# An RWKV block with cross attention on one Trainium2 core: the four-token sums summed over channels into one row set, and the last group's output stage written as two streams

## The chip, the core and the metric

The kernel runs on one core of one Trainium2 chip (trn2). Its engines are TensorE (PE: matmuls, with the weight load PEld as a row of its own), VectorE (DVE), ScalarE (ACT), GpSimd (POOL) and SyncE (SP), whose queue issues every DMA of this kernel. The metric is the device time of one execution in microseconds. Before the change the median of three runs is 973.72 us (974.0, 972.84, 973.72).

## The reference, cut to what matters

Sixteen sequences of 128 tokens with 512 channels go through an RWKV block, 32 heads of 16 channels each, and its output through a small attention over a context:

```python
xa = _ln(x, ln1_w, ln1_b)
sx = concat([state[:, 1:2] - xa[:, :1], xa[:, :-1] - xa[:, 1:]], axis=1)
...
def step(s, rkvw):                       # 128 steps, state s: 16x16 per head
    r_t, k_t, v_t, w_t = rkvw
    a = k_t[..., :, None] * v_t[..., None, :]
    out = jnp.einsum('bhi,bhij->bhj', r_t, u * a + s)
    s = a + w_t[..., :, None] * s
    return (s, out)
...
og = ((og - m) / jnp.sqrt(va + 1e-05)).reshape(b, l, e) * gn_w + gn_b
x1 = x + og * g @ Wo.T
xc = _ln(x1, ln2_w, ln2_b)
sx2 = concat([state[:, 0:1] - xc[:, :1], xc[:, :-1] - xc[:, 1:]], axis=1)
xk2 = xc + sx2 * ffn_maa_k
xr2 = xc + sx2 * ffn_maa_r
rr = jax.nn.sigmoid(xr2 @ Wfr.T)
kk = jnp.square(jax.nn.relu(xk2 @ Wfk.T))
x2 = x1 + rr * (kk @ Wfv.T)
# second layer, x_c = x2, x_s = the context, per sequence:
Mn = conv1x1(Wn, bn, inorm(x_c));  Mm = conv1x1(Wm, bm, inorm(x_s))
A = softmax(einsum('bct,bcs->bts', Mn, Mm))
out = conv1x1(Wo, bo, einsum('bcs,bts->bct', conv1x1(Wl, bl, x_s), A)) + x_c
```

## The kernel before

Everything is fp32; a matmul or a weight load shows as two records in the trace, a transpose on TensorE as one. The 16 sequences form 8 groups (`G`) of two batch elements (`n`), b = 0 and 1. A group passes through stages written as Python generators: `stageB` (first norm, token shift), `stageB2` (the projections k, w, v, r, g), `stageR` (the recurrence), `stageC` (output product with Wo, second norm, the products with Wfk, Wfr, Wfv) and `stageL` (the attention, two generators `stageLb`, one for each b). `stageX` loads the prepared context (MV). Lines 764 to 773 run steps 0 to 11: in a step several groups stand in different stages (`OFF`), and `interleave` (L742) draws one piece at a time from the stream with the smallest key, delay (`DLY`) plus pieces drawn over pieces counted; `NEED` holds a stream back until named stages of its group are drawn. The order drawn is a priority: a scheduler behind it puts each engine's instructions, SP's DMA issues included, in a fixed order before the run, and on the chip every engine and every queue goes through its own order. So an instruction that waits holds up what is queued behind it on its engine.

**The recurrence.** `stageR` holds the 128 tokens in four blocks of 32. For every group and b, `pairs(b)` (L393 to L415) makes the products r times k of tokens within blocks of four: six VectorE products go into `PP` [128 channels, 4, 516], where the four channel blocks cc hold 8 heads each. L405 then sums the 16 channels of each head: one matmul for each cc with the constant `emat` as weights (128 rows by 32 columns, of which 8 are heads) and 512 columns of `PP`; cc's result lies in rows 32cc to 32cc+31 of `pq`, so only 8 of each 32 rows are used. L407 copies `pq` on ScalarE (128x512), L410 transposes it in four pieces of 128x128, and L412 writes it with four masked copies (one for each cc, 128x256) into the score matrix `am`. Three levels follow (`LEV`), with matmuls `pl` at L456 (32 output rows each, in four column groups of the array) and masked copies at L460 (128x512). `spread` and the `Sx` products (L489 to L493) use the same `emat` as a mask of heads. Each b's output is `y[:, b]` (L542), its sums of squares `var[:, b]` (L545). L548 to L557 make the inverse deviations of both b together: 3 + 12 small instructions and one product over 128x1024.

**The output stage.** `stageC` (L566) works on both b at once: SP loads x and the weights (`wpair`: two halves of 512 KB for each weight, tag `wc`, two buffers, so the next weight's half can only be loaded when the matmuls that use this one are through), transposes y (L578), scales it (L580), multiplies by the gate (L582). `tokmajor` (L587) runs the products with Wo, Wfr, Wfv: four matmuls of 128x512 for each b (L592). The sums into x are at L597 and L639, the second norm in `rownorm` (L141 to L145) and L205 to L208, the shifts at L609 and L150. The product with Wfk (L619) has the weight as the stationary operand and both b's tokens, 256 columns, moving. All of it uses the PSUM tag `c` (two banks). The x tile has two buffers, so x of group 7 can be loaded when group 5 is stored (L726).

**The attention.** `stageLb` (L691) makes for each of four token blocks: scores `pS` (L704), maximum (L706), exponential (L708), reciprocal (L709), scaling (L710), four transposes into `pA` (L713), a copy into `AT` (L716, one buffer for everything, two token blocks side by side), and after every second block the product `pO` (L722, 4 matmuls of 128x256) and the sum into x (L724); at the end it stores x (L726). The last group (g = 7) has the PSUM tags `c`, `lv`, `bx`, `ls`, `la` to itself by turns: scores of b = 0 in `c` and of b = 1 in `lv`, `pO` of b = 0 in `lv`.

In step 10 `stageC` of group 7 runs beside `stageL` of group 6; in step 11 `stageL` of group 7, both b, stands alone.

Of the kernel before, what the change touches and what calls it, by code (L numbers as in the profile page):

```python
# [7 lines left out]
FP = mybir.dt.float32  # L8
FPR = mybir.dt.float32r
I32 = mybir.dt.int32  # L10
AF = mybir.ActivationFunctionType
ALU = mybir.AluOpType
AX = mybir.AxisListType

B, L, E, H, S = 16, 128, 512, 32, 16
EPS = 1e-5
(V_LN1W, V_LN1B, V_MAAX, V_TD, V_U, V_GNW, V_GNB, V_LN2W, V_LN2B, V_FMK, V_FMR) = range(11)
NV = 11
n = 2
G = B // n  # L20
# [14 lines left out]
def rwkv_xattn_kernel(ctx: ExitStack, tc: tile.TileContext, a: dict, out: bass.AP):  # L35
# [28 lines left out]
    def loadxn(g):  # L64

        t = [sb.tile([128, 512], FP, name="xn") for _ in range(n)]
        for b in range(n):
# [6 lines left out]
    st = load("st", [128, 2, 4, B])  # L74
    w1 = load("maa_w1", [128, 4, 160])

    LATE = dict(td_w1=[128, 4, 64], td_w2=[128, 512], l1b=[128, 4], emat=[128, 32],
                lvm=[128, 3, 16], dgm=[128, 32])
    late = {k: const.tile(v, I32 if k in ("lvm", "dgm") else FP, name=k) for k, v in LATE.items()}
    td1, td2, l1b, emat, lvm, dgm = late.values()  # L80
# [41 lines left out]
    D = {}  # L122
# [235 lines left out]
    def stageR(g):  # L358
# [34 lines left out]
        def pairs(b):  # L393
            tt = lambda o, x, y: nc.vector.tensor_tensor(o, x, y, ALU.mult)  # L394
            tt(dg[:, :, :, 0:128:4], four(ru, b, 0, 4), four(k, b, 0, 4))
            tt(dg[:, :, 0:3, 1:129:4], four(r, b, 1, 3), four(k, b, 0, 3))
            kw = (sb if last else sb1).tile([128, 4, 2, 32], FP, name="kw", tag="xm" if last else "sq")
            tt(kw, four(k, b, 0, 2), four(w, b, 1, 2))
            tt(dg[:, :, 0:2, 2:129:4], four(r, b, 2, 2), kw)
            tt(kw[:, :, 0], kw[:, :, 0], w[:, :, b, 2:128:4])  # L400
            tt(dg[:, :, 0, 3:129:4], r[:, :, b, 3:128:4], kw[:, :, 0])

            pq = ps.tile([128, 512], FP, name="pq", **P())
            for cc in range(4):
                nc.tensor.matmul(pq[32 * cc : 32 * cc + 32], lhsT=emat, rhs=PP[:, cc, 0:512], start=True, stop=True)  # L405
            pc = sb1.tile([128, 512], FP, name="pc4", tag="gt" if last else "kt")
            nc.scalar.copy(pc, pq)  # L407
            p4 = ps.tile([128, 4, 4, 32], FP, name="p4", **P())
            for q in range(4):
                nc.tensor.transpose(p4[:, q].rearrange("p c h -> p (c h)"), pc[:, 128 * q : 128 * q + 128], ident)  # L410
            for cc in range(4):
                nc.vector.copy_predicated(  # L412
                    am[b][:, 8 * cc : 8 * cc + 8].rearrange("p h (q s) -> p h q s", s=4),
                    dgm.rearrange("p (q s) -> p q s", s=4)[:, None].to_broadcast([128, 8, 8, 4]),
                    p4[:, :, cc, 0:8].rearrange("p s h -> p h s")[:, :, None].to_broadcast([128, 8, 8, 4]))  # L415

        def expand(li):

# [52 lines left out]
        for b in range(n):  # L471
# [14 lines left out]
            def spread(c, src):  # L486

                o = Sx[:, c].rearrange("p m (a q) j -> p m a q j", a=2)
                own = emat[:, 0:8].rearrange("p (a q) -> p a q", a=2)[:, None, :, :, None].to_broadcast([128, 4, 2, 4, 16])  # L489
                nc.vector.tensor_tensor(o, src, own, ALU.mult)  # L490

            nc.vector.tensor_tensor(Sx[:, 0], s0[:, b, :, None, :].to_broadcast([128, 4, 8, 16]),
                                    emat[:, None, 0:8, None].to_broadcast([128, 4, 8, 16]), ALU.mult)  # L493
            vb = vt[:, b].rearrange("p (q x j) -> p x q j", q=4, x=8)
            yield

# [48 lines left out]
            nc.vector.tensor_reduce(var[:, b], sq.rearrange("p (h j) -> p h j", j=16), AX.X, ALU.add)  # L545
            yield

        v, t, rs = (small.tile([128, n, 32], FP, name=q, bufs=1) for q in ("gv", "gt", "gr"))  # L548
        nc.vector.tensor_scalar(v, var, 1.0 / S, EPS, ALU.mult, ALU.add)
        nc.vector.tensor_scalar(t.bitcast(I32), v.bitcast(I32), 1, None, ALU.logical_shift_right)  # L550
        nc.vector.tensor_scalar(rs.bitcast(I32), t.bitcast(I32), -1, 0x5F3759DF, ALU.mult, ALU.add)
        for _ in range(4):
            nc.vector.tensor_tensor(t, rs, rs, ALU.mult)
            nc.vector.scalar_tensor_tensor(t, t, -0.5, v, ALU.mult, ALU.mult)
            nc.vector.scalar_tensor_tensor(rs, t, 1.5, rs, ALU.add, ALU.mult)
        y4 = y.rearrange("p b (h j) -> p (b h) j", j=16)
        nc.vector.tensor_tensor(y4, y4, rs.rearrange("p b h -> p (b h)")[:, :, None].to_broadcast([128, n * 32, 16]), ALU.mult)  # L557
        d["y"] = y
        yield

# [5 lines left out]
    def stageC(g):  # L566
# [73 lines left out]
            d["ssum"][b] = su  # L640

        tokmajor("Wfv", kk, use_f)
        yield


# [107 lines left out]
                done.add(s[4])  # L753

    ST = [(stageB, 3), (stageB2, 5), (stageR, 30), (stageC, 5), (stageL, 6), (stageX, 2)]
    NEED = [(), (0,), (1,), (2,), (3, 5), (), ()]
    done = set()

    def step_of(k, g):
        if k == 5 and g == G - 1:  # L760
            return g + LASTX
        return g + OFF[k]

    for step in range(G + max(OFF)):
        streams = []
        for k in ORDER:
            for g in range(G):
                if step_of(k, g) == step:
                    streams.append((ST[k][0](g), ST[k][1], DLY[k], (k, g)))
        if step in EARLY:  # L770
            gs = EARLY[step]
            streams.append((stageE(gs), 2 * len(gs), 1, (6, step)))
        interleave(streams)


def _prep(np, inp):
# [36 lines left out]
    r["l1b"] = np.stack([L1("bn"), L1("bm"), L1("bl"), L1("bo")], axis=1)  # L813
    r["ident"] = np.eye(128, dtype=np.float32)
    p = np.arange(128)
    r["emat"] = (p[:, None] // 16 == np.arange(32)).astype(np.float32)
    t = p % 32
    q = np.arange(16)
    lv = []
# [25 lines left out]
```

## Time and profile before

The profiled execution took 975.34 us; from its first to its last instruction there are 973.4 us.

| what | profile of before |
|---|---|
| runs | 974.0, 972.84, 973.72 us, median 973.72 |
| profiled execution, span | 975.34 us, 973.4 us |
| instructions | 19141 |
| PE busy / PEld busy | 900.7 us (93%) / 615.9 us (63%) |
| DVE / ACT / POOL busy | 640.3 / 500.4 / 60.2 us |
| mean granted clock of TensorE | 0.977 |
| moved by DMA | 129.83 MB, mean 133 GB/s |

Busy time is the union of an engine's records; a matmul's record runs until its result is out, which overlaps the next matmul in a dense row (eight 128x512 records that start 0.43 us apart take 3.60 us together). A row that says "128*32 128x512" is a weight of 128 rows and 32 columns with 512 moving columns. Times such as 883.3 are microseconds from the start of the span.

### The profile page before, as it was taken

To read this page: it belongs to the slowest core of one execution; us is meant where nothing else is said; L and a number is where in the kernel's file an instruction comes from. 1 tells how busy PE (TensorE), PEld (TensorE's weight loads), DVE (VectorE), ACT (ScalarE), POOL (GpSimd) and SP (SyncE) were. 2 spreads that over 40 slices of the span, in tenths; PEclk is the share of its full clock that TensorE was granted. 3 is DMA by queue.
4 is the path that set the end of the run, shared out by engine and by line. 5 is a ranking of instruction groups with operands and counts; after the bars stand their busy time and mean duration, and the time that the engine had idled before them with its cause. 6 is when DMAs were issued, how large, how long until landed. Compare 5 with 4: busy or idle time off the path is not lost.

```text
span 973.4 us, 19141 instructions
## 1 busy us (share of the span) xinstructions
PE 900.7 (93%) x7524; PEld 615.9 (63%) x7524; DVE 640.3 (66%) x1573; ACT 500.4 (51%) x1053; POOL 60.2 (6%) x94
## 2 busy tenths in 40 slices
PE   3889999999989999999999999999989998988976
PEld 2666767667545867576757676576747665745544
DVE  4697687947586668775887579656774695643221
ACT  4675273443367454564565456635464365654462
POOL 5111010000000000010000000000000000000000
PEclk9999999999999999999999999999999999999996
DMA  6577757365413645253445533643445323242200
GB/s 177 185 241 210 208 158 242 100 156 189 143 55 86 203 126 165 60 172 116 137 122 139 173 99 115 177 145 101 139 118 156 111 71 115 78 122 95 87 22 22
DMA packets 76459, 129.83 MB, mean 133 GB/s; under 512 B 33697, under 2 KB 43553, under 8 KB 76368
## 3 DMA queue, kind: packets, MB, share of 16 engines
q1 hardware_dynamic: 76370, 128.62, 43.7%
q8 instruction: 59, 0.97, 0.4%
q14 instruction: 30, 0.25, 0.1%
HBM read 100.25 MB, written 22.04 MB: 126 GB/s over the span
## 4 chain that ended last, share of the span: by engine, by line
PE 64%; DVE 18%; ACT 7%; DMA 6%; SPq 4%; issue 2%; POOL 0%; DVEq 0%; ACTq 0%; POOLq 0%
PE ptk L592 14%; PE pj L224 11%; PE pj L619 6%; PE pv L331 5%; PE pO L722 5%; PE pl L456 4%; PE pS L704 4%; DVE PP L394 3%; SPq L425 3%; PE pA L713 2%; PE p L245 2%; DVE xm L289 2%; PE pu L505 2%; PE po L533 1%; DVE xm L290 1%
## 5 line engine op out<-in xcount | busy, mean ns | idle before, releaser
L224 PE MATMUL pj<-xm,wb 128*128 128x256 f32 x768 | 179.3, 386 | 3.0 <-DVE xm L289 3.0
L224 PEld LDWEIGHTS pj<-xm,wb 128*128 128x128 f32 x768 | 145.2, 193 | 28.5 <-issue 5.7
L143 POOL TENSOR_TENSOR rs<-rs,mhalf 128x1 f32<-128x1 f32 x64 | 41.9, 660 | 613.1 <-DVE rs L128 550.8
L706 DVE TENSOR_REDUCE nm<-pS 128x1 f32<-128x512 f32 x64 | 44.0, 690 | 47.8 <-PE pS L704 47.5
L708 ACT ACTIVATE e<-pS,nm 128x512 f32<-128x512 f32 x64 | 44.4, 693 | 52.9 <-DVE nm L706 52.6
L704 PE MATMUL pS<-MV,Mn 128*128 128x512 f32 x112 | 59.8, 616 | 7.3 <-ACT e L708 2.8
L619 PE MATMUL pj<-xk,wb 128*128 128x256 f32 x256 | 59.4, 382 | 0.0
L289 DVE TENSOR_TENSOR xm<-px,sx 128x512 f32<-128x512 f32 x80 | 53.7, 683 | 8.5 <-PE px L286 8.4
L592 PE MATMUL ptk<-wb,kk 128*128 128x512 f32 x128 | 58.6, 595 | 0.5 <-DMA wb<-in_Wfv_dram 0.5
L592 PE MATMUL ptk<-wb,sx 128*128 128x512 f32 x128 | 58.1, 598 | 0.3 <-DMA wb<-in_Wfr_dram 0.3
L331 PE MATMUL pv<-wb,xm 128*128 128x512 f32 x128 | 57.5, 597 | 0.6 <-DMA wb<-wvc 0.6
L592 PE MATMUL ptk<-wb,yT 128*128 128x512 f32 x128 | 56.9, 596 | 1.0 <-DVE yT L582 0.9
L722 PE MATMUL pO<-AT,MV 128*128 128x256 f32 x224 | 55.3, 383 | 2.1 <-ACT AT L716 1.9
L710 ACT ACTIVATE e<-e,nm 128x512 f32<-128x512 f32 x64 | 46.5, 729 | 18.8 <-DVE nm L709 18.7
L290 DVE TENSOR_TENSOR xm<-xm,xaT 128x512 f32<-128x512 f32 x80 | 54.4, 685 | 0.5
L716 ACT COPY AT<-pA 128x512 f32<-128x512 f32 x64 | 37.4, 584 | 31.4 <-PE pA L713 28.6
L722 PEld LDWEIGHTS pO<-AT,MV 128*128 128x128 f32 x224 | 41.3, 190 | 17.9 <-issue 6.5
L713 PEld LDWEIGHTS pA<-ident,e 128*128 128x128 f32 x256 | 32.2, 149 | 32.2 <-issue 14.3
L619 PEld LDWEIGHTS pj<-xk,wb 128*128 128x128 f32 x256 | 47.4, 190 | 7.8 <-issue 1.4
L713 PE MATMUL pA<-ident,e 128*128 128x128 f32 x256 | 43.1, 292 | 9.3 <-ACT e L710 5.7
L456 PE MATMUL pl<-KX,r 128*32 128x128 f32 x1536 | 48.6, 274 | 2.7 <-DMA KX<-ks 2.4
L456 PEld LDWEIGHTS pl<-KX,r 128*32 128x32 f32 x1536 | 40.7, 110 | 13.5 <-issue 8.5
(173 smaller groups left out, 1653.3 us busy)
## 6 DMA issues: line engine op xcount, KB each, us to landing
wb<-in_Wk_dram SPq DMA_DIRECT2D x16, 512.0 KB, 4.7
mvD<-MVe SPq DMA_DIRECT2D x16, 512.0 KB, 4.2
wb<-in_Wr_dram SPq DMA_DIRECT2D x16, 512.0 KB, 3.5
wb<-wvc SPq DMA_DIRECT2D x16, 512.0 KB, 3.6
wb<-in_Wg_dram SPq DMA_DIRECT2D x16, 512.0 KB, 4.3
wb<-in_Wo_dram SPq DMA_DIRECT2D x16, 512.0 KB, 3.5
wb<-in_Wfk_dram SPq DMA_DIRECT2D x16, 512.0 KB, 3.6
wb<-in_Wfr_dram SPq DMA_DIRECT2D x16, 512.0 KB, 3.9
```

The source lines that it names most:

```text
L224: nc.tensor.matmul(pj[:, m], lhsT=wb[:, m, cc, :], rhs=xm[:, cc], start=cc == 0, stop=cc == 3)
L289: nc.vector.tensor_tensor(xm[:, sl], px.rearrange("p c (b t) -> p c b t", b=n), sx[:, sl], ALU.mult)
L290: nc.vector.tensor_tensor(xm[:, sl], xm[:, sl], xaT[:, sl, :, 1:129], ALU.add)
L331: nc.tensor.matmul(pv, lhsT=xm[:, m, b], rhs=wbs[m // 2][:, m % 2], start=m == 0, stop=m == 3)
L456: nc.tensor.matmul(t[cs, 128 * cc : 128 * cc + 128], lhsT=r[:, cc, b, cs], rhs=KX[:, n * cc + b, :, 16 * c : 16 * c + 16], start=True, sto ...
L592: nc.tensor.matmul(pt, lhsT=act[:, m, b], rhs=wbs[m // 2][:, m % 2], start=m == 0, stop=m == 3)
L619: nc.tensor.matmul(pj[:, m], lhsT=wb[:, m, cc, :], rhs=xk2[:, cc], start=cc == 0, stop=cc == 3)
L704: nc.tensor.matmul(pS, lhsT=Mn[:, tsl], rhs=Mm, start=True, stop=True)
L708: nc.scalar.activation(e, pS, AF.Exp, bias=nm[:, 0:1], accum_out=nm[:, 1:2])
L710: nc.scalar.activation(e, e, AF.Identity, scale=nm[:, 2:3])
L713: nc.tensor.transpose(pA[:, sc], e[:, 128 * sc : 128 * sc + 128], ident)
L722: nc.tensor.matmul(pO, lhsT=Vc[:, sc], rhs=AT[:, sc], start=sc == 0, stop=sc == 3)
```

## The change

In `pairs`, the weights become windows of a wider constant (56 columns, the heads in columns 24 to 31): for channel block cc the window starts at 24 - 8cc, so its 8 heads land in rows 8cc to 8cc+7. The four cc are accumulated into one tile of 128x128, with the four tokens q of a block in the four row sets of 32. The copy, the transposes and the masked copies then are one each. Where `emat` served as a mask, the columns 24 to 31 are taken.

The inverse deviations of the last group are made for each b by itself. `stageC` and `stageL` of group 7 are no longer drawn; in step 10 four streams take their place, `stageCb` and `stageLb` for each b. `stageCb` is `stageC` for one b: its own PSUM tag (`c`, `lv`), its own weight buffers (`wc`, `wb`) and its own loads of Wo, Wfk, Wfr, Wfv. `NEED` draws `stageCb` of b = 1 after that of b = 0, and `stageLb` of each b after its `stageCb`.

```diff
--- before.py
+++ after.py
@@ -74,7 +74,7 @@
     st = load("st", [128, 2, 4, B])
     w1 = load("maa_w1", [128, 4, 160])
 
-    LATE = dict(td_w1=[128, 4, 64], td_w2=[128, 512], l1b=[128, 4], emat=[128, 32],
+    LATE = dict(td_w1=[128, 4, 64], td_w2=[128, 512], l1b=[128, 4], emat=[128, 56],
                 lvm=[128, 3, 16], dgm=[128, 32])
     late = {k: const.tile(v, I32 if k in ("lvm", "dgm") else FP, name=k) for k, v in LATE.items()}
     td1, td2, l1b, emat, lvm, dgm = late.values()
@@ -400,19 +400,19 @@
             tt(kw[:, :, 0], kw[:, :, 0], w[:, :, b, 2:128:4])
             tt(dg[:, :, 0, 3:129:4], r[:, :, b, 3:128:4], kw[:, :, 0])
 
-            pq = ps.tile([128, 512], FP, name="pq", **P())
+            pq = ps.tile([128, 128], FP, name="pq", **P())
             for cc in range(4):
-                nc.tensor.matmul(pq[32 * cc : 32 * cc + 32], lhsT=emat, rhs=PP[:, cc, 0:512], start=True, stop=True)
-            pc = sb1.tile([128, 512], FP, name="pc4", tag="gt" if last else "kt")
+                for q in range(4):
+                    nc.tensor.matmul(pq[32 * q : 32 * q + 32], lhsT=emat[:, 24 - 8 * cc : 56 - 8 * cc],
+                                     rhs=PP[:, cc, 128 * q : 128 * q + 128], start=cc == 0, stop=cc == 3)
+            pc = sb1.tile([128, 128], FP, name="pc4", tag="gt" if last else "kt")
             nc.scalar.copy(pc, pq)
-            p4 = ps.tile([128, 4, 4, 32], FP, name="p4", **P())
-            for q in range(4):
-                nc.tensor.transpose(p4[:, q].rearrange("p c h -> p (c h)"), pc[:, 128 * q : 128 * q + 128], ident)
-            for cc in range(4):
-                nc.vector.copy_predicated(
-                    am[b][:, 8 * cc : 8 * cc + 8].rearrange("p h (q s) -> p h q s", s=4),
-                    dgm.rearrange("p (q s) -> p q s", s=4)[:, None].to_broadcast([128, 8, 8, 4]),
-                    p4[:, :, cc, 0:8].rearrange("p s h -> p h s")[:, :, None].to_broadcast([128, 8, 8, 4]))
+            p4 = ps.tile([128, 4, 32], FP, name="p4", **P())
+            nc.tensor.transpose(p4.rearrange("p s h -> p (s h)"), pc, ident)
+            nc.vector.copy_predicated(
+                am[b].rearrange("p h (q s) -> p h q s", s=4),
+                dgm.rearrange("p (q s) -> p q s", s=4)[:, None].to_broadcast([128, 32, 8, 4]),
+                p4.rearrange("p s h -> p h s")[:, :, None].to_broadcast([128, 32, 8, 4]))
 
         def expand(li):
 
@@ -486,11 +486,11 @@
             def spread(c, src):
 
                 o = Sx[:, c].rearrange("p m (a q) j -> p m a q j", a=2)
-                own = emat[:, 0:8].rearrange("p (a q) -> p a q", a=2)[:, None, :, :, None].to_broadcast([128, 4, 2, 4, 16])
+                own = emat[:, 24:32].rearrange("p (a q) -> p a q", a=2)[:, None, :, :, None].to_broadcast([128, 4, 2, 4, 16])
                 nc.vector.tensor_tensor(o, src, own, ALU.mult)
 
             nc.vector.tensor_tensor(Sx[:, 0], s0[:, b, :, None, :].to_broadcast([128, 4, 8, 16]),
-                                    emat[:, None, 0:8, None].to_broadcast([128, 4, 8, 16]), ALU.mult)
+                                    emat[:, None, 24:32, None].to_broadcast([128, 4, 8, 16]), ALU.mult)
             vb = vt[:, b].rearrange("p (q x j) -> p x q j", q=4, x=8)
             yield
 
@@ -545,16 +545,18 @@
             nc.vector.tensor_reduce(var[:, b], sq.rearrange("p (h j) -> p h j", j=16), AX.X, ALU.add)
             yield
 
-        v, t, rs = (small.tile([128, n, 32], FP, name=q, bufs=1) for q in ("gv", "gt", "gr"))
-        nc.vector.tensor_scalar(v, var, 1.0 / S, EPS, ALU.mult, ALU.add)
-        nc.vector.tensor_scalar(t.bitcast(I32), v.bitcast(I32), 1, None, ALU.logical_shift_right)
-        nc.vector.tensor_scalar(rs.bitcast(I32), t.bitcast(I32), -1, 0x5F3759DF, ALU.mult, ALU.add)
-        for _ in range(4):
-            nc.vector.tensor_tensor(t, rs, rs, ALU.mult)
-            nc.vector.scalar_tensor_tensor(t, t, -0.5, v, ALU.mult, ALU.mult)
-            nc.vector.scalar_tensor_tensor(rs, t, 1.5, rs, ALU.add, ALU.mult)
-        y4 = y.rearrange("p b (h j) -> p (b h) j", j=16)
-        nc.vector.tensor_tensor(y4, y4, rs.rearrange("p b h -> p (b h)")[:, :, None].to_broadcast([128, n * 32, 16]), ALU.mult)
+        for bs in ([slice(b, b + 1) for b in range(n)] if last else [slice(0, n)]):
+            k_ = bs.stop - bs.start
+            v, t, rs = (small.tile([128, k_, 32], FP, name=q, bufs=1) for q in ("gv", "gt", "gr"))
+            nc.vector.tensor_scalar(v, var[:, bs], 1.0 / S, EPS, ALU.mult, ALU.add)
+            nc.vector.tensor_scalar(t.bitcast(I32), v.bitcast(I32), 1, None, ALU.logical_shift_right)
+            nc.vector.tensor_scalar(rs.bitcast(I32), t.bitcast(I32), -1, 0x5F3759DF, ALU.mult, ALU.add)
+            for _ in range(4):
+                nc.vector.tensor_tensor(t, rs, rs, ALU.mult)
+                nc.vector.scalar_tensor_tensor(t, t, -0.5, v, ALU.mult, ALU.mult)
+                nc.vector.scalar_tensor_tensor(rs, t, 1.5, rs, ALU.add, ALU.mult)
+            y4 = y[:, bs].rearrange("p b (h j) -> p (b h) j", j=16)
+            nc.vector.tensor_tensor(y4, y4, rs.rearrange("p b h -> p (b h)")[:, :, None].to_broadcast([128, k_ * 32, 16]), ALU.mult)
         d["y"] = y
         yield
 
@@ -640,6 +642,85 @@
             d["ssum"][b] = su
 
         tokmajor("Wfv", kk, use_f)
+        yield
+
+    def stageCb(g, b):
+
+        d = D[g]
+        tag = ("c", "lv")[b]
+        if b == 0:
+            d["x"] = loadx(g)
+            d["ssum"] = [None, None]
+            d["gt"] = sb.tile([128, 4, n, 128], FP, name="gt2l", tag="xm")
+            nc.sync.dma_start(out=d["gt"], in_=d["gD"])
+            for nm, tg in (("yT", "yT"), ("sx2", "sx2"), ("xk2", "xk2"), ("kk", "gt")):
+                d[nm] = sb1.tile([128, 4, n, 128], FP, name=nm + "l", tag=tg)
+            d["xcT"] = sb1.tile([128, 4, n, 129], FP, name="xcTl", tag="xcT")
+        xb = d["x"][b]
+        yT, sx2, xk2, kk = (d[nm][:, :, b] for nm in ("yT", "sx2", "xk2", "kk"))
+        xT = d["xcT"][:, :, b]
+
+        def weight(nm):
+            r = []
+            for m2 in range(2):
+                t = sb.tile([128, 2, 512], FP, name="wl", tag=("wc", "wb")[b], bufs=2)
+                nc.sync.dma_start(out=t, in_=a[nm][m2])
+                r.append(t)
+            return r
+
+        def tok(act, wbs):
+            pt = ps.tile([128, 512], FP, name="ptl", **T(tag))
+            for m in range(4):
+                nc.tensor.matmul(pt, lhsT=act[:, m], rhs=wbs[m // 2][:, m % 2], start=m == 0, stop=m == 3)
+            return pt
+
+        wo = weight("Wo")
+        pt = ps.tile([128, 4, 128], FP, name="pyl", **T(tag))
+        for m in range(4):
+            nc.tensor.transpose(pt[:, m], d["y"][:, b, 128 * m : 128 * m + 128], ident)
+        for m in range(4):
+            nc.scalar.activation(yT[:, m], pt[:, m], AF.Identity, bias=vec[:, V_GNB, m : m + 1],
+                                 scale=vec[:, V_GNW, m : m + 1])
+        nc.vector.tensor_tensor(yT, yT, d["gt"][:, :, b], ALU.mult)
+        yield
+        su = small.tile([128, 1], FP, name="su2")
+        nc.vector.scalar_tensor_tensor(xb, tok(yT, wo), 1.0, xb, ALU.mult, ALU.add, accum_out=su)
+        wk = weight("Wfk")
+        yield
+        t = sb.tile([128, 512], FP, name="xn")
+        rownorm(t, xb, "ln", "act", su)
+        nc.gpsimd.tensor_copy(xT[:, :, 0], st[:, 0, :, n * g + b])
+        pt = ps.tile([128, 4, 128], FP, name="ptn", **T(tag))
+        for c in range(4):
+            nc.tensor.transpose(pt[:, c], t[:, 128 * c : 128 * c + 128], ident)
+        for c in range(4):
+            nc.scalar.activation(xT[:, c, 1:129], pt[:, c], AF.Identity, bias=vec[:, V_LN2B, c : c + 1],
+                                 scale=vec[:, V_LN2W, c : c + 1])
+        xc = xT[:, :, 1:129]
+        nc.vector.tensor_tensor(sx2, xT[:, :, 0:128], xc, ALU.subtract)
+        axpb(xk2, sx2, V_FMK, xc)
+        axpb(sx2, sx2, V_FMR, xc)
+        yield
+        pj = ps.tile([128, 4, 128], FP, name="pjl", **T(tag))
+        for m in range(4):
+            wb = wk[m // 2].rearrange("p m (c f) -> p m c f", c=4)
+            for cc in range(4):
+                nc.tensor.matmul(pj[:, m], lhsT=wb[:, m % 2, cc, :], rhs=xk2[:, cc], start=cc == 0, stop=cc == 3)
+        nc.scalar.activation(kk, pj, AF.Relu)
+        nc.scalar.activation(kk, kk, AF.Square)
+        wr = weight("Wfr")
+        yield
+        p = tok(sx2, wr)
+        nc.scalar.activation(sx2, p.rearrange("p (c t) -> p c t", c=4), AF.Tanh, scale=0.5)
+        nc.scalar.activation(sx2, sx2, AF.Identity, scale=0.5, bias=halft)
+        wv = weight("Wfv")
+        yield
+        p = tok(kk, wv)
+        nc.vector.tensor_tensor(sx2, sx2, p.rearrange("p (c t) -> p c t", c=4), ALU.mult)
+        xv = xb.rearrange("p (c t) -> p c t", c=4)
+        su = small.tile([128, 1], FP, name="su3")
+        nc.vector.scalar_tensor_tensor(xv, sx2, 1.0, xv, ALU.mult, ALU.add, accum_out=su)
+        d["ssum"][b] = su
         yield
 
 
@@ -753,7 +834,7 @@
                 done.add(s[4])
 
     ST = [(stageB, 3), (stageB2, 5), (stageR, 30), (stageC, 5), (stageL, 6), (stageX, 2)]
-    NEED = [(), (0,), (1,), (2,), (3, 5), (), ()]
+    NEED = [(), (0,), (1,), (2,), (3, 5), (), (), (2,), (2, 7), (7, 5), (8, 5)]
     done = set()
 
     def step_of(k, g):
@@ -763,9 +844,13 @@
 
     for step in range(G + max(OFF)):
         streams = []
+        if step == G + 2:
+            for b in range(n):
+                streams.append((stageCb(G - 1, b), 6, 0.4 + 0.1 * b, (7 + b, G - 1)))
+                streams.append((stageLb(G - 1, b), 3, 1.4 + 0.1 * b, (9 + b, G - 1)))
         for k in ORDER:
             for g in range(G):
-                if step_of(k, g) == step:
+                if step_of(k, g) == step and not (g == G - 1 and k in (3, 4)):
                     streams.append((ST[k][0](g), ST[k][1], DLY[k], (k, g)))
         if step in EARLY:
             gs = EARLY[step]
@@ -813,7 +898,7 @@
     r["l1b"] = np.stack([L1("bn"), L1("bm"), L1("bl"), L1("bo")], axis=1)
     r["ident"] = np.eye(128, dtype=np.float32)
     p = np.arange(128)
-    r["emat"] = (p[:, None] // 16 == np.arange(32)).astype(np.float32)
+    r["emat"] = (p[:, None] // 16 == np.arange(56) - 24).astype(np.float32)
     t = p % 32
     q = np.arange(16)
     lv = []
```

## The prediction

> **What bounds it now.** I read the page's busy times and its chain of waits first, then the granted clock and busy time by stretches, then the groups of the lines that the diff touches, then the order in time of the last 100 us.
>
> ```profile
> PE 900.7 (93%) x7524; PEld 615.9 (63%) x7524; DVE 640.3 (66%) x1573; ACT 500.4 (51%) x1053; POOL 60.2 (6%) x94
> PE 64%; DVE 18%; ACT 7%; DMA 6%; SPq 4%; issue 2%; POOL 0%; DVEq 0%; ACTq 0%; POOLq 0%
> ```
>
> Over the whole span TensorE is the bound, and the chain runs through it for 64%. By stretches (start:end and length, busy us of PE, PEld, DVE, ACT, POOL, then granted clock, DMA share, GB/s) there are two regimes:
>
> ```profile
> 500.00:600.00 100.00, 99.71 (x896) 69.51 (x896) 71.95 (x174) 55.25 (x120) 4.05 (x8) 1.00 0.44 133
> ...
> 868.00:884.00 16.00, 12.78 (x44) 6.92 (x44) 3.25 (x8) 6.43 (x16) 0.55 (x1) 1.00 0.56 177
> 884.00:904.00 20.00, 16.46 (x65) 12.23 (x66) 9.21 (x27) 13.47 (x27) 1.10 (x2) 0.91 0.18 58
> 904.00:924.00 20.00, 19.11 (x58) 9.59 (x56) 5.63 (x16) 8.78 (x18) 0.55 (x1) 1.00 0.23 70
> 924.00:944.00 20.00, 15.34 (x58) 9.17 (x56) 6.94 (x17) 12.44 (x26) 0.55 (x1) 1.00 0.07 27
> 944.00:974.00 30.00, 19.38 (x52) 12.61 (x52) 3.48 (x9) 9.67 (x20) 0.00 (x0) 0.64 0.05 17
> ```
>
> In the middle PE is full: only less PE work helps there. From 868 on it is idle for 22.9 us (106.0 - 83.1), and in the last 30 us it runs at a granted clock of 0.64. There the bound is a chain of dependent work.
>
> **Part 1, the sums over channels (16 times, 8 groups by 2).** Columns: line, engine, operation, operands, shapes, count | busy us, mean ns | idle before.
>
> ```profile
> L456 PE MATMUL pl<-KX,r 128*32 128x128 f32 x1536 | 48.6, 274 | 2.7 <-DMA KX<-ks 2.4 <-DVE AM L412 0.4
> L460 DVE COPY_PREDICATED AM<-lvm,pl 128x512 f32<-128x512 int32 x42 | 29.4, 711 | 12.2 <-PE pl L456 11.9
> L405 PE MATMUL pq<-PP,emat 128*32 128x512 f32 x128 | 17.9, 633 | 2.0 <-DVE PP L394 1.9
> L410 PE MATMUL p<-ident,pc 128*128 128x128 f32 x64 | 9.9, 277 | 0.0
> L412 DVE COPY_PREDICATED AM<-dgm,p 128x256 f32<-128x256 int32 x56 | 20.1, 441 | 0.0
> L249 PE MATMUL p<-xq,maa_w 128*32 128x64 f32 x256 | 6.6, 222 | 0.0
> ```
>
> Matmuls: now 8 records of 512 columns, 17.9/16 = 1.12 us; then 32 records of 128 columns with 24 more weight loads. L456 is this form, 32 records in 48.6/48 = 1.01 us. L249 accumulates over cc in four column sets just as the new code does, 32 records in 6.6/8 = 0.82 us, so accumulating costs nothing that shows. I take 1.01: 0.11 less. Transposes: four in 9.9/16 = 0.62 us, one in 0.28: 0.34 less (0.33 by the 0.11 us step of a dense row, 0.44 us for four on the chain). PE saves 0.33 to 0.45 a time, 5.3 to 7.2 in all; its share of the chain, 64%, gives 3.4 to 4.6 us. VectorE: 4 x 0.441 = 1.76 us become one copy of 1024 columns. No row has a masked copy that long; it lies between 1.22 (L557, a product over 1024) and 1.76, and from 256 to 512 columns L412 and L460 add 0.27, so 0.71 + 2 x 0.27 = 1.25 is nearest. It saves 0 to 0.54 a time, 0 to 8.6 in all, times 18%: up to 1.5, by 1.25 us 1.5. ScalarE: 0.585 becomes 0.28 (L303, a 128x128 activation alone) to 0.48 (L580): 1.7 to 4.9 in all, times 7%: 0.1 to 0.3. Sum 3.5 to 6.4, I take **-5**. At best the whole 7.2 of PE counts. At worst the new order of instructions, which I can't see, costs a stretch: from 200 to 300 us PE is idle 8.5 us, against 1.1 per 100 us from 300 to 700, so +7.
>
> **Part 2, the tail.** First the edits at no cost. The deviations of the last group come twice: 15 small instructions more, of 0.2 us, 3 us of VectorE. They fit in front of L545 at 859.05, where VectorE had stood idle for 9.57 us; without that cover they would cost 3 us, though only up to x: x of group 7 waits for group 5's store (875.43) and lands just before 883.34, and products of both b are ready by then. So an earlier y of b = 0 buys nothing, and 15 us of slack lie between y and x.
>
> ```profile
> 875.43 0.34 SPq L726 DMA_DIRECT2D out_dram<-x  x1
> 879.46 0.38 SPq L61 DMA_DIRECT2D x<-in_x_dram  x1
> ...
> 883.34 0.69 DVE L597 SCALAR_TENSOR_TENSOR x<-ptk,x 128x512 f32<-128x512 f32 x1 [7.93 <-DMA x<-in_x_dram]
> ...
> 894.88 7.07 PE L619 MATMUL pj<-xk,wb 128*128 128x256 f32 x32
> ```
>
> *Norm and shift.* Before, b = 0 waits for b = 1: 11.5 us from 883.34 to 894.88. Alone, b = 0 has its scaled x at 887.7 (norm of 886.9 plus 0.8), then 4 transposes 0.6, 4 activations at 0.36 (L580: 8 in 2.90) 1.45, the subtraction 0.69, four sums of 128 columns at 0.29 to 0.39 (L385, L394) 1.2 to 1.6: 891.6. Its product with Wfk starts 3.3 us earlier.
>
> *Products.* Work on PE stays: Wfk for one b is 32 records of 128 columns with full weights, and L665 has 8 of that form in 0.89 us, so 3.55 instead of 3.53 (half of 7.07). From 894.88 to the last product, 919.7, 24.8 us pass with group 6's pieces in them; the same from 891.6 gives 916.4, and the sums end at about 918.2 for b = 1 instead of 922.87: **-4.6**. For b = 0, done one product sooner, about 914.5 instead of 921.16.
>
> *Weights.* Eight halves more, 4.2 MB; a half lands in about 3.6 us, so 29 us of transfers, in a stretch with a DMA share of 0.19. Hidden if the other stream's 3.5 us of product covers the 1.8 us by which a load outlasts the product's second half; uncovered it is 1.8 for each of 6 products. But SP works in order: if Wo of b = 1 is queued behind the MV load that waits until 874.84, the store and the x load, it goes out at 880.9 and lands at 884.5, its product ends at 888 and b = 1 is 4.2 late. So -4.6 to -0.4; I take **-3**, since SP is free from 854.4 to 863 and the `wb` buffers are free from 855.4 (last transposes of `am`).
>
> *Attention of group 7.* From x of b = 1 (922.87) to the end it takes 50.5 us. The products `pO` share the one `AT`:
>
> ```profile
> 937.62 1.99 PE L722 MATMUL pO<-AT,MVl 128*128 128x256 f32 x8 [0.67 <-ACT AT L716]
> ...
> 948.01 3.62 PE L722 MATMUL pO<-AT,MVl 128*128 128x256 f32 x8
> ...
> 954.10 3.78 PE L722 MATMUL pO<-AT,MVl 128*128 128x256 f32 x8 [0.68 <-ACT AT L716]
> 957.67 2.70 PE L704 MATMUL pS<-MVl,Mn 128*128 128x512 f32 x4
> ...
> 966.17 3.65 PE L722 MATMUL pO<-AT,MVl 128*128 128x256 f32 x8 [0.68 <-ACT AT L716]
> ```
>
> The steps are 10.4, 6.1 and 12.1 us. 6.1 is what the ring needs at this clock: copy 0.59, transposes 1.12, copy 0.58, product 3.7. The 12.1 has the scores of b = 1's last two blocks queued behind the third product, whose bank (`lv`) they share; now the streams are drawn block by block, and b = 0 is 4 us ahead. Both long steps at 6.1 would give -10.3; if nothing changes, 0. I take **-7**, two thirds, as the cause of the longest step is what the new drawing order changes.
>
> A rule speaks against this part. The Trainium skill, "TensorE: Matmul & The Clock Gate", "Why this matters for your kernels", says that after gaps of some 3 us without work the array falls back to half clock. The trace agrees: the same `pO` takes 1.99 at 937.62 and 3.6 to 3.8 after the idle of 2.80 us at 944.13. By the rule a stream left alone at the end runs its whole 9.5 us of PE work (`pn` 0.86, `pS` 3.43, `pA` 1.73, `pO` 3.46) at half rate, +9.5 against the full clock; before, 30 us at 0.64 lost 19.4 x 0.36 = 7.0 already, so by the rule the sum would be 2.5 higher.
>
> **Sum.** 973.4 - 5 - 3 - 7 = 958.4. The median shown is 0.3 above this span (973.72; the profiled execution itself took 975.34): **958.7 us**.
>
> **Rivals.** *The tail keeps its end* (0.19): group 6's last `pO` at 932.43 still holds `AT`, x of b = 1 is only 0.4 earlier, the steps stay; what is left is part 1, 968.7. For it: ScalarE, VectorE and PSUM are asked for the same work. Against it: b = 0 no longer waits for b = 1. *Full overlap* (0.14): part 1 at -7.2, x of b = 1 at -4.6, steps at 6.1: 973.7 - 22.1 = 951.6, and down to 944 if b = 0's products get out ahead of 932. For it: 22.9 us of idle PE; against it: one `AT`. *Slower* (0.15): on SP each stream's load stands behind the other's waiting one, so every product waits for its own load. From 891.6 six products of 3.5 + 3.6 end at 934.2, x of b = 1 at 936; b = 0, one product earlier, at 929, has its first `pO` 13.8 later (norm 3.9, `pn` and copy 1.8, `pS` 1.0, two blocks on ScalarE 4.6, `pA` and `AT` 2.5) at 942.8, and 2.6 more as an array that has stood idle runs `pn`, `pS` and `pA` at half its rate (as `pO` at 948.01); with the old steps 28.6 and 7.2 from the last `pO` to the end that is 981.2, 976.2 after part 1, **976.5** as a median. It decides from x of b = 1 at about 934. For it: L215 is the largest wait on SP now; against it: at 903.56 a load that outlasted its cover cost PE only 0.32.
>
> **From cases to chances.** The forecast has 0.52 and its own range 951 to 966 (part 1 -7 to -3, the tail's two terms -15 to -5). 0.2%, 1.9 us, is about what a measurement of this kernel tells from no change. Faster: 0.52 + 0.14 + 0.17 of the tail's rival; same: 0.02 of it and 0.04 of the slower case; slower 0.11. The range goes from the full overlap's low end to where the slower case starts: 944 to 974.
>
> **What would show it.** L405's successor at about 1.0 us a time and PE busy some 6 us lower up to 868; one masked copy near 1.25 us; x of group 7 still near 883; the first Wfk product of group 7 near 891.6, x of b = 1 near 918 to 920; steps of the last `pO` near 7. I am wrong if the second stream's Wo lands after x, if PE in the middle is less full than 98%, or if the last stream stands alone for over 25 us.

## The result, and the profile after

The changed kernel takes **982.4 us** (median of 17 runs, 976.15 to 986.64) beside 974.29 us for the kernel before on the same chips (17 runs, 969.78 to 980.54): ratio 1.0075, 95% interval 1.0056 to 1.0093. It is 0.75% slower, some 7 us, where -15 us was predicted. The profiled execution took 982.66 us, 980.9 from first to last instruction (before 973.4).

The busy times and the chain of waits of the changed kernel:

```profile
PE 903.5 (92%) x7892; PEld 622.3 (63%) x7892; DVE 644.3 (66%) x1551; ACT 495.4 (51%) x1057; POOL 62.8 (6%) x95
PE 66%; DVE 18%; DMA 6%; ACT 5%; SPq 2%; issue 2%; POOL 1%; DVEq 0%; ACTq 0%; POOLq 0%
```

TensorE's busy time did not fall; it is 2.8 us higher. The groups of the new instructions (busy us, mean ns of one record):

```profile
L406 PE MATMUL pq<-PP,emat 128*32 128x128 f32 x512 | 21.5, 295 | 4.4 <-DVE PP L394 4.4
...
L412 DVE COPY_PREDICATED AM<-dgm,p 128x1024 f32<-128x1024 int32 x14 | 18.2, 1297 | 0.0
...
L411 PE MATMUL p<-ident,pc 128*128 128x128 f32 x16 | 4.8, 303 | 0.0
...
L409 ACT COPY pc<-pq 128x128 f32<-128x128 f32 x16 | 4.4, 278 | 2.2 <-PE pq L406 2.2
```

The copy (1.30 us), the one transpose (0.30) and ScalarE's copy (0.28) are what was predicted. The sums take 21.5/16 = 1.34 us a time, not 1.01: 3.6 us more busy time than before (17.9) instead of 1.8 less.

Where the time went shows in stretches of 20 us in the middle, which I had taken for full. Before (columns as in the prediction; the clock stands before the last two numbers):

```profile
180.00:200.00 20.00, 18.18 (x153) 11.19 (x152) 16.51 (x32) 10.21 (x25) 1.13 (x1) 1.00 0.38 90
220.00:240.00 20.00, 17.57 (x122) 14.44 (x121) 16.14 (x39) 5.71 (x11) 1.97 (x3) 0.91 0.56 186
280.00:300.00 20.00, 17.16 (x65) 7.57 (x65) 16.37 (x40) 14.60 (x35) 0.00 (x0) 0.91 0.10 14
400.00:420.00 20.00, 20.00 (x151) 11.51 (x150) 12.95 (x39) 11.49 (x32) 1.70 (x3) 1.00 0.40 91
```

After:

```profile
180.00:200.00 20.00, 14.85 (x114) 9.52 (x107) 17.71 (x31) 8.08 (x23) 1.73 (x1) 0.83 0.13 40
...
220.00:240.00 20.00, 15.95 (x164) 12.94 (x163) 17.35 (x43) 10.65 (x28) 1.10 (x2) 0.83 0.58 196
280.00:300.00 20.00, 15.81 (x135) 10.33 (x134) 19.67 (x48) 10.99 (x29) 1.48 (x2) 0.83 0.13 39
400.00:420.00 20.00, 14.60 (x82) 8.55 (x82) 16.78 (x28) 12.30 (x31) 0.59 (x1) 0.83 0.15 42
```

TensorE stands idle up to 5.4 us in such a stretch, VectorE is busier in each, and the granted clock is at 0.83. From 100 to 868 us TensorE idles 36.8 us instead of 27.2. One such gap, TensorE of the changed kernel in order of time (start, us, and in brackets the idle time before and what ended it):

```profile
408.90 1.08 PE L406 MATMUL pq<-PP,emat 128*32 128x128 f32 x32
409.92 0.66 PE L794 MATMUL pA<-ident,e 128*128 128x128 f32 x4
413.94 0.79 PE L286 MATMUL px<-sk,w2s 98*128 98x256 f32 x2 [3.37 <-ACT w L312]
...
415.17 3.62 PE L594 MATMUL ptk<-wb,yT 128*128 128x512 f32 x4
```

and ScalarE in the same stretch:

```profile
409.19 1.49 ACT L582 ACTIVATE yT<-py,vec 128x128 f32<-128x128 f32 x4
410.56 1.15 ACT L312 ACTIVATE w<-pw,vec 128x128 f32<-128x128 f32 x4
411.56 1.55 ACT L582 ACTIVATE yT<-py,vec 128x128 f32<-128x128 f32 x4
412.93 0.95 ACT L312 ACTIVATE w<-pw,vec 128x128 f32<-128x128 f32 x3
```

TensorE's next product `px` waits until ScalarE has been through eight scalings of yT (L582) and the decays w (L312); then the four products of yT (L594) take 3.62 us, where four of the same form take 1.88 at 917.95. The kernel before has TensorE full in the same 20 us. Neither the products that wait here nor what they wait for is in the diff: what changed is which instruction stands beside which.

The tail, TensorE's stretches and the products `pO` of group 7 in the changed kernel:

```profile
954.00:981.00 27.00, 15.96 (x63) 10.50 (x62) 5.73 (x14) 11.05 (x23) 0.00 (x0) 0.92 0.05 20
```

```profile
955.48 1.99 PE L803 MATMUL pO<-AT,MVl 128*128 128x256 f32 x8 [0.68 <-ACT AT L797]
...
961.73 1.37 PE L794 MATMUL pA<-ident,e 128*128 128x128 f32 x8 [2.54 <-ACT e L791]
963.06 3.52 PE L803 MATMUL pO<-AT,MVl 128*128 128x256 f32 x8
...
968.59 1.99 PE L803 MATMUL pO<-AT,MVl 128*128 128x256 f32 x8 [0.68 <-ACT AT L797]
970.42 1.02 PE L785 MATMUL pS<-MVl,Mn 128*128 128x512 f32 x2
973.99 0.66 PE L794 MATMUL pA<-ident,e 128*128 128x128 f32 x4 [2.55 <-ACT e L791]
975.32 1.99 PE L803 MATMUL pO<-AT,MVl 128*128 128x256 f32 x8 [0.68 <-ACT AT L797]
```

Their steps are 7.6, 5.5 and 6.7 us (before 10.4, 6.1, 12.1), and the clock in the last stretch is 0.92 instead of 0.64. But the tail begins late. SyncE's queue in the changed kernel:

```profile
890.09 0.33 SPq L768 DMA_DIRECT2D MV<-mvD  x1
891.19 0.34 SPq L807 DMA_DIRECT2D out_dram<-x  x1
895.93 0.38 SPq L61 DMA_DIRECT2D x<-in_x_dram  x1
```

The load of x of group 7 goes out at 895.93, 16.5 us later than before (879.46). From it to the end it takes 85.0 us, before 93.9. So 16.5 are lost ahead of it and 8.9 won behind it: +7.6, the 7.5 between the two spans.

### The profile page after: what moved, and what is told of

Its sections match the earlier page's. It is cut to its first block, busy times and chain, and to the rows that moved or that the text cites. A ratio compares the mean times of both kernels' runs of the same rounds, so it can differ in the third digit from the quotient of the medians.

```text
span 980.9 us, 19899 instructions
## 1 busy us (share of the span) xinstructions
PE 903.5 (92%) x7892; PEld 622.3 (63%) x7892; DVE 644.3 (66%) x1551; ACT 495.4 (51%) x1057; POOL 62.8 (6%) x95
## 4 chain that ended last, share of the span: by engine, by line
PE 66%; DVE 18%; DMA 6%; ACT 5%; SPq 2%; issue 2%; POOL 1%; DVEq 0%; ACTq 0%; POOLq 0%
PE ptk L594 13%; PE pj L224 12%; PE pv L331 6%; PE pj L621 5%; PE pO L803 5%; PE pl L456 4%; PE pS L785 4%; DVE PP L394 3%; PE pA L794 2%; DVE xm L289 2%; PE ptl L674 2%; PE po L533 2%; DVE xm L290 2%; SPq L425 1%; PE pa L526 1%
## 5 line engine op out<-in xcount | busy, mean ns | idle before, releaser
L621 PE MATMUL pj<-xk,wb 128*128 128x256 f32 x224 | 52.1, 381 | 0.0
L594 PE MATMUL ptk<-wb,kk 128*128 128x512 f32 x112 | 51.3, 596 | 0.6 <-DMA wb<-in_Wfv_dram 0.6
L594 PE MATMUL ptk<-wb,yT 128*128 128x512 f32 x112 | 51.9, 618 | 0.0
L456 PEld LDWEIGHTS pl<-KX,r 128*32 128x32 f32 x1536 | 40.7, 110 | 17.4 <-issue 11.5
L594 PE MATMUL ptk<-wb,sx 128*128 128x512 f32 x112 | 51.3, 598 | 0.0
L794 PE MATMUL pA<-ident,e 128*128 128x128 f32 x256 | 41.3, 282 | 10.3 <-ACT e L791 8.3
L794 PEld LDWEIGHTS pA<-ident,e 128*128 128x128 f32 x256 | 30.2, 143 | 30.0 <-ACT e L791 13.7
L286 PE MATMUL px<-sk,w2s 98*128 98x256 f32 x160 | 41.3, 357 | 7.2 <-ACT w L312 4.5
```

The costliest lines, as they stand in the source:

```text
L456: nc.tensor.matmul(t[cs, 128 * cc : 128 * cc + 128], lhsT=r[:, cc, b, cs], rhs=KX[:, n * cc + b, :, 16 * c : 16 * c + 16], start=True, sto ...
L594: nc.tensor.matmul(pt, lhsT=act[:, m, b], rhs=wbs[m // 2][:, m % 2], start=m == 0, stop=m == 3)
L621: nc.tensor.matmul(pj[:, m], lhsT=wb[:, m, cc, :], rhs=xk2[:, cc], start=cc == 0, stop=cc == 3)
L794: nc.tensor.transpose(pA[:, sc], e[:, 128 * sc : 128 * sc + 128], ident)
```

## The experiments

Ratios are to the kernel before, run beside each on the same chip, with the 95% interval. "Sums" is part 1, "streams" part 2. Executions of one kernel spread by about 1% (before: 969.78 to 980.54 us) and a profile is one of them, so a time inside a profile can be some us off the middle of its kernel.

### One part alone

*Sums alone*: the kernel before with the hunks of `emat`, `pq`, `pc`, `p4` and the masked copy.

> The kernel before with the new sums alone (one accumulated tile, one transpose, one masked copy); the last output stage as before. Theory A (the loss lies ahead of the tail: the new sums make the scheduler put the instructions of every group in another, worse order): 8 to 18 us slower than before, about 982 to 992. Theory B (the two streams of the last group do the harm): 3 to 7 us faster than before, 967 to 971, as forecast for this part.

Measured: 996.21 us, **1.0216** (1.0177 to 1.0255). The sums alone cost more than the whole change. TensorE's busy time is 909.9 us, the granted clock 0.965, the load of x goes out at 893.23 (+13.8), and from there to the end it takes 101.7 us (before 93.9).

*Streams alone*: the other hunks.

> The kernel before with the two output streams of the last group alone; the sums as before. The order of instructions is that of before up to the tail on every engine. Theory A: faster by the 5 to 12 us that the tail gained between the load of x of group 7 and the end (in the changed kernel 82 us instead of 91): 962 to 969. Theory B: 5 to 12 us slower than before, 979 to 986.

Measured: 973.11 us, 0.9972 (0.994 to 1.0003), span 968.7. Little or nothing is won (the interval still holds 1), where -10 was predicted. So the loss comes with the sums; in the order that the sums bring, the streams take 14 us off (994.9 to 980.9 between the spans).

### What of the sums does it

*Sums with the masked copy in four pieces of 256 columns*, as before, on the new `p4`:

```diff
-            nc.vector.copy_predicated(
-                am[b].rearrange("p h (q s) -> p h q s", s=4),
-                dgm.rearrange("p (q s) -> p q s", s=4)[:, None].to_broadcast([128, 32, 8, 4]),
-                p4.rearrange("p s h -> p h s")[:, :, None].to_broadcast([128, 32, 8, 4]))
+            for cc in range(4):
+                nc.vector.copy_predicated(
+                    am[b][:, 8 * cc : 8 * cc + 8].rearrange("p h (q s) -> p h q s", s=4),
+                    dgm.rearrange("p (q s) -> p q s", s=4)[:, None].to_broadcast([128, 8, 8, 4]),
+                    p4[:, :, 8 * cc : 8 * cc + 8].rearrange("p s h -> p h s")[:, :, None].to_broadcast([128, 8, 8, 4]))
```

> As the first of these runs, but the masked copy of 1024 columns is made in four of 256 again. Theory A: another order again, so anything from 968 to 992, not tied to the length of the copy. Theory C (one long copy blocks VectorE for 1.3 us while PE waits for it): it recovers most of the loss of the first run, 970 to 976.

Measured: 1012.72 us, 1.039 (1.0351 to 1.043), outside both ranges. This prices no copy: the scheduler made yet another order of instructions for it (TensorE's sequence departs from that of the sums alone at the 270th instruction). It shows that a small edit here moves the time by percents.

*The first two products of `pairs` exchanged in the kernel before*:

```diff
-            tt(dg[:, :, :, 0:128:4], four(ru, b, 0, 4), four(k, b, 0, 4))
...
+            tt(dg[:, :, :, 0:128:4], four(ru, b, 0, 4), four(k, b, 0, 4))
```

> The kernel before with the first two of the six products of the sums in the other order; on the other engines the order stays. Theory A in its strong form (any small change of order costs 10 us): off by more than 5 us. Otherwise the same within 3 us: then it takes a rearrangement of whole groups.

Measured: 974.21 us, 1.0 (0.9968 to 1.0032). The lines come out in the same order on TensorE and VectorE, so this says nothing on the order.

Now the order itself. In the kernel before TensorE has 4194 instructions in its queue; with the sums alone the order departs from it at the 191st, VectorE's at the 178th of 1541 (a subtraction of the token shift is put ahead of the products of `pairs`). With the streams alone it departs only at the 4010th. An order can be held: at the end of the kernel function each engine's instructions are chained in a given list, by edges that order instructions of one engine and wait for nothing.

```diff
+    keep_order(tc, nc)
...
+        for p, q in zip(order, order[1:]):
+            tc.add_manual_dep(line[q], line[p].name, info, reason="keep_order")
```

*The sums, all five engines held to the order of the kernel before* (the new matmuls of a cc in place of the old one of that cc, the one transpose and copy in place of the last of four):

> The new sums alone, but every engine and every queue is held to the order of instructions of the kernel before (the new matmuls, the transpose and the masked copy stand where the old ones stood). Theory A (the order does the harm, the new instructions themselves cost less): 967 to 973, that is 1 to 6 us faster than before. Theory C (the new instructions cost more than the rows let one think): 985 to 996, as slow as with their own order.

Measured: 974.11 us, **1.0024** (0.9993 to 1.0054): no loss, but not the 1 to 6 us of gain either.

*The instructions of the kernel before, in the order of the sums alone*:

> The instructions of the kernel before, held to the order that the new sums alone gave. Theory A: 988 to 1002, slow as the first run of the study (996) or a little slower, though not one instruction of the old kernel is changed. Theory C: 971 to 977, as before.

Measured: 1002.08 us, **1.0304** (1.0266 to 1.0342). This is the cross that settles it: the order costs 3.0% without any of the new instructions, and the new instructions cost nothing that can be told without the order. The chains themselves are no rival: they add no waiting instruction (the run before this one has 812 semaphore instructions in its trace, the kernel before 819), and with them on all five engines that run comes out at 1.0024. The same 20 us, first in the sums held to the old order, then in the old sums in the new order:

```profile
400.00:420.00 20.00, 20.00 (x148) 11.05 (x146) 12.96 (x37) 11.34 (x31) 1.70 (x3) 1.00 0.33 102
```

```profile
400.00:420.00 20.00, 14.54 (x90) 8.52 (x89) 17.88 (x42) 10.68 (x28) 0.00 (x0) 1.00 0.36 103
```

The gap goes with the order. And the pages' first lines, in the same sequence:

```profile
PE 892.6 (92%) x7860; PEld 619.1 (64%) x7860; DVE 638.7 (66%) x1525; ACT 494.5 (51%) x1053; POOL 58.1 (6%) x94
```

```profile
PE 921.6 (92%) x7524; PEld 622.8 (62%) x7524; DVE 642.9 (64%) x1573; ACT 500.6 (50%) x1053; POOL 61.8 (6%) x94
```

With the new sums held to the old order TensorE's busy time is 8.1 us below 900.7. The rows of the new instructions account for 5.1 of it (the transposes 9.9 to 4.6, the sums 17.9 to 18.1); the profile also has a higher granted clock, 0.982 beside 0.977. The old instructions in the new order raise it by 20.9, at a granted clock of 0.964. There L405 has 26.1/16 = 1.63 us a time where it had 1.12.

*Both parts, held to the order of the streams alone*:

> Both parts of the change, held to the order that the two streams with the old sums gave (e2). Theory A: the streams' 973 less what the sums save by themselves, 1 to 6: 966 to 972, faster than both kernels. Theory C: 985 or more.

Measured: 972.03 us, 1.0026 (0.9995 to 1.0056): no gain over the streams alone (0.9972).

### Which engine's order

Each is the sums alone, with only the named engines held to the order of before. For the others the scheduler makes an order anew, so they don't keep that of the sums alone; where two of the expectations below say that they keep it, they are wrong.

> The new sums alone, VectorE alone held to the old kernel's order; the scheduler chooses the order of the other engines. If the harm lies in VectorE's order, where the products of the sums and the mixing for the next group compete: 968 to 978. If it lies elsewhere: 988 or more.

> The same with TensorE alone held to the old order. If the harm lies in TensorE's order (what stands behind a matmul that waits): 968 to 978. If it lies elsewhere: 988 or more. Both this and the run before fast: either order draws the other after it.

> The new sums alone; TensorE and VectorE are held to the order that the kernel before has, ScalarE, SyncE and GpSimd keep the order of the new sums alone (1.0216). Theory A, the order of TensorE and VectorE together carries the loss: 1.00 to 1.006. Theory B, ScalarE's order carries it, as ScalarE's exp of w stood in front of the activations that TensorE waited for: 1.015 or more.

> The same with ScalarE held too; only SyncE and GpSimd keep the new order. Theory A and B both: 1.00 to 1.006, as with all five held (1.0024). If SyncE's order of loads and stores carries the loss: 1.015 or more.

> The new sums alone; only ScalarE is held to the order of before. Theory A: no gain, 1.015 to 1.03. Theory B: 1.00 to 1.008.

> The new sums alone; only SyncE is held to the order of before. If SyncE's order of loads and stores carries the loss: 1.00 to 1.008. Theory A and B both: 1.015 to 1.03.

| held to the order of before | us | ratio |
|---|---|---|
| none | 996.21 | 1.0216 (1.0177 to 1.0255) |
| VectorE | 998.45 | 1.0243 (1.0212 to 1.0275) |
| TensorE | 990.39 | 1.0152 (1.0113 to 1.0192) |
| ScalarE | 999.18 | 1.0279 (1.0229 to 1.0329) |
| SyncE | 1008.16 | 1.0362 (1.0318 to 1.0405) |
| TensorE and VectorE | 978.22 | 1.0056 (1.0033 to 1.008) |
| TensorE, VectorE and ScalarE | 976.6 | 1.0037 (1.0003 to 1.0071) |
| all five | 974.11 | 1.0024 (0.9993 to 1.0054) |

None of these four queues, held alone, brings the time back (GpSimd was not tried alone); TensorE and VectorE together bring back about three quarters (2.16% to 0.56%). But a held queue draws the others along. A count from the traces shows how far: the fewest instructions that would have to be moved to have the order of before, instructions being told apart by line and tiles. (TensorE's matmul records, 7860, are 1576 off with none held, 454 with VectorE held and 479 with ScalarE held.)

| held | VectorE, of 1493 | ScalarE, of 956 | SyncE, of 533 |
|---|---|---|---|
| none | 433 | 233 | 67 |
| VectorE | 0 | 58 | 20 |
| TensorE | 65 | 27 | 4 |
| ScalarE | 180 | 0 | 15 |
| SyncE | 430 | 253 | 0 |
| TensorE and VectorE | 0 | 11 | 3 |

So with TensorE and VectorE held, ScalarE is nearly back in the old order by itself, and that run doesn't separate the three: which queue carries the loss isn't shown. My reading of the gap at 410, that ScalarE's order is to blame, is neither shown nor refuted: ScalarE held alone helps nothing, but VectorE then has an order of its own. What is shown is how little it takes: with TensorE in the old order and the other three off it by 65, 27 and 4 instructions, 1.5% is still lost. SyncE put right alone is the slowest of the table (1.0362 beside 1.0216); VectorE and ScalarE are then as far from the old order as with none held.

### The tail

*The streams, with x of the last group in a buffer of its own* (one that the decays `w` leave free), so that its load need not wait until group 5 is stored:

```diff
-        x = xpool.tile([128, n, 512], FP, name="x")
+        x = sb1.tile([128, n, 512], FP, name="xl", tag="w") if g == G - 1 else xpool.tile([128, n, 512], FP, name="x")
```

> The two streams with the old sums; x of the last group has a buffer of its own (that of w, which is done by then) and needn't wait for the store of group 5. If this wait is what the streams lost their gain to (x came at 884 instead of 879 and x of b = 1 was done at 928 instead of 923): 961 to 969. If PE or ScalarE are the bound there anyway: 971 to 976.

Measured: 957.09 us, **0.9848** (0.9809 to 0.9886), better than forecast. The same edit in the kernel before:

> The kernel before with the buffer of its own for x of the last group, and nothing else. If the early x alone made e8 fast: 955 to 961. If it takes the two streams to use it: 966 to 972, since the joint attention phase of group 7 still takes its 50 us.

Measured: 971.88 us, 0.9966 (0.9935 to 0.9996). The buffer alone is worth 0.3%, the streams alone 0.3% (not clear of noise), together 1.5%: each waits for what the other removes. Why shows in TensorE's order in the streams alone:

```profile
868.02 3.88 PE L674 MATMUL ptl<-wl,yTl 128*128 128x512 f32 x8 [0.16 <-DVE yTl L684]
871.74 1.02 PE L785 MATMUL pS<-MV,Mn 128*128 128x512 f32 x2
872.60 3.60 PE L674 MATMUL ptl<-wl,yTl 128*128 128x512 f32 x8
...
877.33 1.97 PE L803 MATMUL pO<-AT,MV 128*128 128x256 f32 x8
```

and in the kernel before:

```profile
872.92 1.89 PE L722 MATMUL pO<-AT,MV 128*128 128x256 f32 x8
875.00 7.13 PE L592 MATMUL ptk<-wb,yT 128*128 128x512 f32 x16 [0.19 <-DVE yT L582]
```

The streams have the products with Wo ready early, so they stand ahead of group 5's last `pO`, which starts 4.4 us later. Its sum, its store (879.85 instead of 875.43) and the load of x (884.39 instead of 879.46) follow. The finished products then wait for x. With x at hand the two sums into it come at once, 14 and 10 us earlier than in the streams alone (888.20 and 888.81). VectorE in the streams with own x:

```profile
874.34 0.69 DVE L687 SCALAR_TENSOR_TENSOR xl<-ptl,xl 128x512 f32<-128x512 f32 x1 [2.09 <-PE ptl L674]
...
878.63 0.69 DVE L687 SCALAR_TENSOR_TENSOR xl<-ptl,xl 128x512 f32<-128x512 f32 x1 [1.55 <-PE ptl L674]
```

*Both parts and the own buffer, held to the order of the streams with own x*:

> Both parts of the change and the own buffer for x, held to the order of e8. Theory A: as e8 within 4 us, 953 to 961, as the new sums by themselves neither gain nor lose (e5, e7).

Measured: 962.05 us, 0.9882 (0.9841 to 0.9923), 1 us outside the range. Again the sums add no gain that can be told. These two runs with x in its own buffer are the fastest of all; their intervals overlap, and so does the span of their profiles (957.0 and 956.9), so which of the two is better isn't shown.

## Why the prediction was wrong

**The step that failed: "its share of the chain, 64%, gives 3.4 to 4.6 us", with the new order of instructions at "+7" at worst.** I summed what the edited instructions save and treated the order as a small risk. It is the whole result: the order by itself is +3.0% (some 30 us at 974), four times my bound, and with the new instructions +2.2%. I had drawn the bound from idle TensorE alone (8.5 us in a bad stretch). The lower clock after the gaps counts too: by the granted clock of the stretches of 100 us from 100 to 868, the shortfall adds up to some 17 us of full speed after and 7 before, beside the 9.6 us of idle. That is an upper bound, since a low clock costs nothing while TensorE idles.

**The terms of part 1.** In the old order the sums take 1.13 us (18.1/16; predicted 1.01, before 1.12), so they save nothing; the transposes, the masked copy and ScalarE's copy came out at 0.29, 1.30 and 0.27 (0.28, 1.25, 0.28). So the new instructions take 5.1 us less of TensorE (5.3 to 7.2 predicted), all of it in the transposes. And yet the time is the same (1.0024): the interval leaves 0.07% of a gain, 0.7 us, where 5 were predicted. In the held order TensorE idles 33.0 us from 100 to 868 instead of 27.2, and the load of x goes out at 880.95 (before 879.46): the 5.8 us by which it is less busy there became idle time. In three pairs the sums with the order held come out 0.2% to 0.5% above the kernel without them (1.0024 beside 1, 1.0026 beside 0.9972, 0.9882 beside 0.9848), none of them clear of noise. In the bad order they do pay: 1.0216 beside 1.0304. My own sign of an error was TensorE less full than 98% in the middle: from 400 to 500 us the changed kernel has 94.60 us (before 98.73). "Only less PE work helps there" was wrong: in the middle, what follows what in the queues decides.

**x of b = 1, -3 predicted.** Two steps failed. One is "x of group 7 still near 883", the assumption that group 5's store does not move. In the streams alone the load is 4.9 us late, the first product with Wfk starts at 900.44 (predicted 891.6, before 894.88), and x of b = 1 is ready at 928.94 instead of 922.87: **+6.1**. Where I listed what "buys nothing" I asked what an earlier y waits for, but not what its products push back. The other is "Its product with Wfk starts 3.3 us earlier". The streams alone:

```profile
888.20 0.69 DVE L687 SCALAR_TENSOR_TENSOR x<-ptl,x 128x512 f32<-128x512 f32 x1 [1.11 <-DMA x<-in_x_dram]
```

```profile
900.44 3.96 PE L708 MATMUL pjl<-xk2l,wl 128*128 128x128 f32 x32
```

From the first sum into x to this product pass 12.2 us; before it was 11.5, and I had added up 8.3 for b = 0 alone, without group 6's pieces, which stand in between on ScalarE and TensorE. To x of b = 1 it takes 40.7 us from there (before 39.5). With x in its own buffer it is 39.1, so x of b = 1 at 913.40, -9.5, is earlier almost only because x is there 9.0 us earlier; the saving of -3 showed in no run.

**The attention, -7 predicted.** From x of b = 1 to the end the streams alone take 39.8 us, the changed kernel 39.3, before 50.5: **-10.7**, just beyond the good end of my range (0 to -10.3). The cause was half right, and the size has luck in it. Before, two blocks of scores stood behind the third product (957.67); in the changed kernel one still does (970.42), as in the streams alone (956.51 behind 954.68). Besides, TensorE's rate is higher: the third product takes 1.99 us where it took 3.78, though the rule that I cited spoke for a lower one.

**The clock rule.** Read from the Trainium skill ("TensorE: Matmul & The Clock Gate", "Why this matters for your kernels"), it would, by my estimate, have made the tail 2.5 us longer. The tail went the other way: a granted clock of 0.92 in the last 27 us, with three of four `pO` at 1.99 us. What the rule says shows where I didn't look, in the middle: after the 3.37 us idle before 413.94 four products take 3.62 instead of 1.88 us.

**The rivals.** The slower one (976.5, by weights that come too late, from x of b = 1 at 934 on) has the right sign and the right sign post (x of b = 1 at 941.63) by the wrong mechanism: TensorE's one wait for a weight in the changed kernel's streams is 0.81 us, in the streams alone 0.16. The true place is the order in the middle, which I had only as an end of a range. The streams alone land near *the tail keeps its end*, but by two terms that cancel, +6.1 and -10.7.

**Open:** why the scheduler's order departs at that place, which queue's order carries the loss, and which pairs of instructions make the gaps. Nor was the sums' order tuned by hand to see whether a third order beats both.

## What to carry to other kernels

An edit that leaves every engine less to do can lose percents if a scheduler reorders the queues behind it. Compare the order before and after, and run the cross (new instructions in the old order, old ones in the new) before any instruction is blamed. When a stage is started earlier, ask which older stage its work now stands ahead of, and whether a buffer that the new stage needs comes from there: here the streams and the free buffer gave 0.3% each, and 1.5% together.

## Not expected of the hardware

The same 32 records of the sums take 1.08 us in a dense stretch (408.90) and 1.34 on the mean of the changed kernel, 1.13 with the order held. Of two waits of 2.54 and 2.55 us in the last stretch, the first was followed by a `pO` of 3.52 us, the second by one of 1.99: such a gap does not always bring the slow rate.
